# Sorted experts: block 0's results are gathered behind the scatters of the third part's rows

## The chip, the cores and the metric

The kernel runs on one core of a Trainium2 chip. The time is the device time of one execution in microseconds. The kernel before was run six times: 3030.4 to 3040.61 us, median 3032.41.

## The reference

Four layers act on 2048 tokens of 128 features. Each layer is a feed-forward part, an attention-like part, and the same feed-forward part again, all with residual sums. The change touches the boundary between layer 1 and layer 2: the second run of layer 1's feed-forward part, a mixture of 8 experts of which each token uses 2, and the feed-forward part of layer 2 that follows it.

```
def _L1_ffn_ref(x, rw1, rb1, rw2, rb2, we1, be1, we2, be2):
    ...
    logits = jax.nn.silu(xt @ rw1 + rb1) @ rw2 + rb2
    _, idx = jax.lax.top_k(logits, K)
    mask = jnp.zeros((n, E), bool).at[jnp.arange(n)[:, None], idx].set(True)
    w = jax.nn.softmax(jnp.where(mask, logits, -jnp.inf), axis=1)
    h = jax.nn.silu(jnp.einsum('nd,edh->enh', xt, we1) + be1[:, None, :])
    eo = jnp.einsum('enh,ehd->end', h, we2) + be2[:, None, :]
    y = xt + jnp.einsum('ne,end->nd', w, eo)
...
x = x + _L1_attn_ref(_layernorm(x, axis=-1), ...)
x = x + 0.5 * _L1_ffn_ref(_layernorm(x, axis=-1), ...)
x = x + 0.5 * _L2_ffn_ref(_layernorm(x, axis=-1), ...)
```

## The kernel before

The residual stream `x` stays in SBUF, features on partitions, as four blocks of 512 tokens. For the second run of layer 1's experts the class `Slots` sorts tokens by expert, so that each expert's tokens fill tiles of 128 rows and only the chosen experts are computed. The blocks form three parts: blocks 0 and 1 (23 tiles), block 2 (15 tiles), block 3 (15 tiles). "The third part" below is block 3; the code counts it as 2.

For each part the steps are these.

- `route` (from L1094 on) normalises a block, finds the two experts of each token and their shares, and turns the rows around (`s_xt`).
- `sort` works out a slot for each token and choice. Its first step adds the two choices (L1148); its second multiplies on TensorE (L1152, L1153); its third and fourth are small DVE operations (L1155 to L1175); its fifth writes the slots as integers (L1183) and issues eight scatters on GpSimd's queue (L1188), which write the rows of `s_xt` into `s_xd` in DRAM; its sixth finds each tile's expert (L1190 to L1194).
- `load` reads `s_xd` back, sorted, with four transfers on SyncE's queue (L1207).
- `body` and `part_of` run the tiles. Each tile has a first product (L1282, four matrix products into `s_h_ps`), a bias addition on DVE (L1287), a SiLU on ACT (L1288), and two tiles later a second product (L1298) into the sum bank `s_y`. There is one sum bank for four tiles; ACT copies it out (L1302) and SyncE stores it into `s_yd` in DRAM (L1303). Ahead of its use, DVE and ACT copy the expert's weights of each tile out of `we` (L1262). Every four tiles PE transposes the loaded rows (L1273) and ACT copies them (L1275).
- `combine(b)` brings the results of block b back to token order: eight gathers on GpSimd's queue (L1333) read `s_yd` into two tiles `s_g`; four transposes on PE (L1338) and a copy on ACT (L1340) turn the shares; 14 yields later DVE multiplies by the shares (L1345) and adds the two choices (L1346); 3 yields later PE multiplies the biases (L1349) and turns the sum (L1352); 2 yields later DVE adds it to `x` (L1355).

The order of all this is written by hand by `Weave`. The class runs a list of bodies (first the three parts of the sorted experts, then the gates and downs of layer 2's experts). After every `yield` of a body a clock advances by one, and `pump` first starts those waiting jobs whose conditions are met and then advances each active job whose time has come by one step. A job's yield of n puts its next step n clocks later, plus the job's slack: 2 by default, 0 where the job was given 0. At most two jobs with default slack run beside a body. The instructions of PE, DVE, ACT and GpSimd go into their queues in exactly the order in which this emits them; SyncE's order is found by the tile framework.

The jobs beside the sorted experts are set up in `in_slots`. `("sort", 0, 2)` is the third part's sort. Behind it come the load of `wg2`, the gate weights of layer 2 (2 MB, named `wg` in the profile, L1845), and `("loaded", 0, 2)`, the loads of the third part's rows. `("combined", 0, b)` is `combine(b)`; block 0's has slack 0. The condition of block 0's is that the body of the first part, `("slots", 0, 0)`, is through; each later block's combine waits also for the one before it. The first head of layer 2, `("head", 0, 0)` (normalisation L122 to L150, router L252 to L257, gate factors stored in DRAM as `rt_cd`), waits for `("combined", 0, 0)`; its factors are then spread by loads of 1 MB each into `f_xs` (L385), one while the sorted experts run and the next when their last buffers are free. DVE scales them (L1879) for the gate products (L1891).

Of the kernel before, what the change touches and what calls it, by code (L numbers as in the profile page):

```python
# [1713 lines left out]
class Behind:  # L1714
# [116 lines left out]
    def in_slots(self, weave):  # L1831

        fl, slots = self.fl, self.slots
        held = lambda name: fl.sp.tile([P, BLK], F32, tag="xn", name=name, bufs=3)
        weave.job(("loaded", 0, 0), [], lambda: slots.load(0, fl))
        weave.job("output", [("loaded", 0, 0)], lambda: self.fa.output(NB - 1, fl.sp, fl.bank, fl.work), 0)

        def load(*names):
            tiles = {name: self.late.tile(list(_SHAPES[name]), F32, tag=name, name=name) for name in names}
            for name, t in tiles.items():  # L1840

                flat = t.rearrange("p a b c -> p (a b c)") if len(t.shape) == 4 else t
                flat = t.rearrange("p a b -> p (a b)") if len(t.shape) == 3 else flat
                self.net.nc.vector.memset(flat[:, 0:1], 0.0)
                self.net.nc.sync.dma_start(t, self.net.ins[name])  # L1845
            self.w.update(tiles)
            return
            yield

        route = lambda: slots.route(3, fl.sp, fl.bank, fl.work, held)  # L1850
        weave.job(("route", 0, 3), ["output"], route, 0)
        weave.job(("loaded", 0, 1), ["output"], lambda: slots.load(1, fl), 0)
        sort = lambda: slots.sort(2, fl.bank, fl.work)
        weave.job(("sort", 0, 2), [("route", 0, 3)], sort, 0)
        weave.job("wg2", [("sort", 0, 2)], lambda: load("wg2"), 0)
        weave.job(("loaded", 0, 2), [("sort", 0, 2)], lambda: slots.load(2, fl), 0)
        weave.job("weights", [("slots", 0, 1)], lambda: load("wu2", "wd2", "rw3", "wg3", "wu3", "wd3", "wout3"), 0)
        weave.job("constants", [("combined", 0, 1)], self.constants)
        for b in range(NB):

            after = [("slots", 0, max(b - 1, 0))] + ([("combined", 0, b - 1)] if b else [])
            weave.job(("combined", 0, b), after, lambda b=b: slots.combine(b, fl), None if b else 0)


# [514 lines left out]
```

## Time and profile before

| | us |
|---|---|
| median of six runs | 3032.41 |
| the profiled execution | 3032.82 |
| its span | 3031.0 |
| PE busy | 2815.2 (93%) |
| DVE busy | 1937.0 (64%) |
| ACT busy | 1308.0 (43%) |
| POOL busy | 111.4 (4%) |
| first product of the second part's tiles (L1282) | starts at 1988.60 |
| slots of the third part written (L1183) | 1995.80, 0.19 long |
| load of `wg` issued (L1845) | 1997.81 |
| loads of the third part's rows issued (L1207) | 2025.79 |
| first product of the third part's tiles (L1282) | starts at 2039.40 |
| first gate product (L1891) | starts at 2081.12 |

Times within the execution count from the start of its span. PE is TensorE, DVE is VectorE, ACT is ScalarE, POOL is GpSimd and SP is SyncE. A row of a timeline gives start, duration, engine, source line, operation, the tile written and the tiles read, how many instructions were merged into it, and in brackets the engine's idle time before it with what ended that idle time. An fp32 matrix product shows as two matmul instructions, so eight stand for four products. A POOL row covers the work of building the transfer's descriptors, not the landing of its data.

### The profile page before, as it was taken

The numbers are of one execution on the slowest core, as the hardware profiler recorded it, in microseconds if no ns is written. First come the engines' busy times: TensorE is split into PE (matmuls) and PEld (weight loads), VectorE is DVE, ScalarE is ACT, GpSimd is POOL, SyncE is SP. The second block draws the span as 40 slices with busy tenths as digits, with TensorE's granted clock in tenths as the row PEclk, the third lists the DMA queues.
The fourth block names the chain that finished last, engine by engine and source line by source line (L and its number), as shares of the span: only waits on it lengthen the run. The fifth ranks groups of instructions, "written<-read, shape, count | busy, mean of one in ns | idle before, by whom it ended". The sixth has DMA issues, their size and how long they took to land.

```text
span 3031.0 us, 33081 instructions
## 1 busy us (share of the span) xinstructions
PE 2815.2 (93%) x12377; PEld 1239.9 (41%) x12404; DVE 1937.0 (64%) x3897; ACT 1308.0 (43%) x1717; POOL 111.4 (4%) x190
## 2 busy tenths in 40 slices
PE   6589999998899989999999999989999999999997
PEld 3234444443444432333333322576444444444443
DVE  4476686764545578999989886345355545553665
ACT  2365454532444425666666767754211122111242
POOL 0110000000000000000000001132000000000000
PEclk9789999998999988999999999989999999999998
DMA  1000100001001000000000001133221111110000
GB/s 51 4 1 1 47 1 1 1 1 58 15 1 42 22 22 15 6 21 17 7 27 6 14 5 39 38 100 138 85 75 65 70 56 70 56 75 37 28 1 15
DMA packets 53601, 101.03 MB, mean 33 GB/s; under 512 B 21572, under 2 KB 39752, under 8 KB 46784
## 3 DMA queue, kind: packets, MB, share of 16 engines
q1 hardware_dynamic: 51392, 94.71, 9.0%
q0 software_dynamic: 2048, 4.20, 0.5%
q8 instruction: 98, 1.61, 0.2%
q14 instruction: 63, 0.52, 0.1%
HBM read 83.35 MB, written 13.89 MB: 32 GB/s over the span
## 4 chain that ended last, share of the span: by engine, by line
PE 77%; DVE 14%; ACT 6%; issue 2%; DMA 1%; SPq 0%; another core or an unknown queue 0%; DVEq 0%; ACTq 0%; POOLq 0%
PE f_h L1891 15%; PE fa_av L1596 8%; PE fa_s L1530 8%; PE fa_s L1607 7%; PE f_y L1953 4%; PE f_y L969 4%; PE f_h_ps L960 3%; PE ga_u L832 3%; PE ga_u L842 3%; PE ga_s L816 3%; DVE fa_mx L1533 2%; PE f_y L521 2%; DVE f_ms L1936 2%; PE ln_c L122 2%; DVE ga_acc L658 1%
## 5 line engine op out<-in xcount | busy, mean ns | idle before, releaser
L1533 DVE TENSOR_REDUCE fa_mx<-fa_s 128x1 f32<-128x512 f32 x1024 | 652.1, 685 | 88.4 <-PE fa_s L1530 86.2
L1615 ACT ACTIVATE fa_ex<-fa_s 128x1024 f32<-128x1024 f32 x512 | 501.1, 1022 | 269.5 <-PE fa_s L1607 264.7
L1530 PE MATMUL fa_s<-fa_ks,fa_qs 75*128 75x512 bf16 x1024 | 366.1, 391 | 16.3 <-DVE fa_mx L1533 7.6
L1607 PE MATMUL fa_s<-fa_qs,fa_ks 75*128 75x512 bf16 x1024 | 308.5, 386 | 8.6 <-ACT fa_ex L1615 7.7
L1596 PE MATMUL fa_av<-fa_ex,fa_v 128*32 128x512 f32 x2048 | 277.4, 613 | 0.0
L1953 PE MATMUL f_y<-f_ms,wd 128*128 128x512 f32 x512 | 238.0, 602 | 12.0 <-DVE f_ms L1936 10.1
L1530 PEld LDWEIGHTS <-fa_qs 75*128 75x128 bf16 x1024 | 100.4, 98 | 316.3 <-issue 234.6
L1891 PE MATMUL f_h<-f_xs,wg 128*128 128x512 f32 x512 | 229.7, 595 | 0.0
L1891 PE MATMUL f_h<-f_xs,wu 128*128 128x512 f32 x512 | 226.2, 594 | 0.0
L1936 DVE TENSOR_TENSOR f_ms<-f_mid,f_xs 128x512 f32<-128x512 f32 x256 | 166.7, 687 | 15.0 <-PE f_y L1953 14.9
L1607 PEld LDWEIGHTS <-fa_ks 75*128 75x128 bf16 x1024 | 99.3, 99 | 133.0 <-issue 55.8
L1953 PEld LDWEIGHTS f_y<-f_ms,wd 128*128 128x128 f32 x512 | 91.6, 190 | 132.9 <-issue 80.0
L963 ACT ACTIVATE f_h<-f_h_ps,vec 128x512 f32<-128x512 f32 x128 | 87.2, 687 | 130.8 <-PE f_h_ps L960 128.0
L827 DVE TENSOR_TENSOR ga_a<-ga_s,ga_e 128x1024 f32<-128x1024 f32 x96 | 117.2, 1221 | 37.6 <-PE ga_s L816 22.1
L1891 PEld LDWEIGHTS f_h<-f_xs,wu 128*128 128x128 f32 x512 | 95.4, 190 | 111.9 <-issue 111.2
L966 DVE TENSOR_TENSOR f_h<-f_h,cb 128x512 f32<-128x512 f32 x128 | 86.0, 684 | 85.9 <-ACT f_h L963 74.5
L1891 PEld LDWEIGHTS f_h<-f_xs,wg 128*128 128x128 f32 x512 | 94.4, 190 | 107.2 <-issue 106.5
L960 PE MATMUL f_h_ps<-ln_xn,we 128*128 128x512 f32 x256 | 130.5, 595 | 1.1 <-DVE fa_f L1443 0.6
L1903 DVE TENSOR_TENSOR f_mid<-f_mid,f_h 128x512 f32<-128x512 f32 x32 | 22.0, 688 | 168.2 <-PE f_h L1891 168.2
L969 PE MATMUL f_y<-f_h,we 128*128 128x512 f32 x256 | 127.8, 593 | 0.0
L832 PE MATMUL ga_u<-ga_a,ga_kv 128*64 128x512 f32 x384 | 119.3, 634 | 3.0 <-DVE ga_state L801 2.0
L842 PEld LDWEIGHTS ga_u<-ga_xe,ga_diag 128*128 128x128 f32 x720 | 88.8, 194 | 75.8 <-issue 75.0
(466 smaller groups left out, 3754.5 us busy)
## 6 DMA issues: line engine op xcount, KB each, us to landing
f_xs<-rt_cd SPq DMA_DIRECT2D x48, 1024.0 KB
fa_ks<-fa_kd SPq DMA_DIRECT2D x48, 96.0 KB
fa_qs<-fa_qd SPq DMA_DIRECT2D x16, 288.0 KB
we<-in_we_dram SPq DMA_DIRECT2D x1, 4112.0 KB
s_x<-s_xd SPq DMA_DIRECT2D x11, 256.0 KB
s_yd<-s_ys SPq DMA_DIRECT2D x11, 256.0 KB
wg<-in_wg_dram SPq DMA_DIRECT2D x1, 2048.0 KB
wu<-in_wu_dram SPq DMA_DIRECT2D x1, 2048.0 KB
```

The costliest lines, as they stand in the source:

```text
L832: nc.tensor.matmul(u_ps[64 * h : 64 * h + 64, :], lhsT=kv[:, i, 2 * p + h, lo : lo + 64], rhs=a[:, h, :], start=True, stop=first, skip_gro ...
L842: nc.tensor.matmul(u_ps[:, r * P : (r + 1) * P], lhsT=now[:, r, int(step == 2), :], rhs=xe[:, r, :], start=False, stop=r == 3, skip_group_ ...
L960: nc.tensor.matmul(h_ps, lhsT=w["we"][:, e, 4 + c * P : 4 + (c + 1) * P], rhs=xn, start=True, stop=True)
L969: nc.tensor.matmul(y, lhsT=w["we"][:, e, 516 + c * P : 516 + (c + 1) * P], rhs=hs[e][:, c, :], start=False, stop=(e, c) == (7, 3),)
L1530: nc.tensor.matmul(s1, lhsT=qs[:, h, i * P : (i + 1) * P], rhs=ks[:, c, h, :], start=True, stop=True)
L1533: nc.vector.tensor_reduce(mx[:, h, i, c : c + 1], s1, AX.X, ALU.max)
L1596: nc.tensor.matmul(av[at], lhsT=v[:, n, at], rhs=exs[j // 2][:, j % 2, :], start=n == 0, stop=n == NT - 1)
L1607: nc.tensor.matmul(s2[:, j, :], lhsT=ks[:, n // 4, h, n % 4 * P : (n % 4 + 1) * P], rhs=qs[:, h, :], start=True, stop=True,)
L1615: nc.scalar.activation(ex, s2, AF.Exp)
L1891: nc.tensor.matmul(ps, lhsT=wt[:, e, c * P : (c + 1) * P], rhs=halves[e // 4][:, e % 4, :], start=e == 0, stop=e == 7,)
L1936: self.net.nc.vector.tensor_tensor(ms, mid[:, c, :], halves[e // 4][:, e % 4, :], ALU.mult)
L1953: nc.tensor.matmul(y, lhsT=self.w["wd2"][:, c, e, :], rhs=ms, start=e == 0 and c == 0, stop=e == 7 and c == 3,)
```

## The change

One condition of one job is added. Block 0's combine is to start only when the third part's sort is through, in addition to the first part's body. The instructions of both are the same; what changes is the order in which they, and those of the jobs that wait for block 0's combine, are put into the queues.

```diff
         for b in range(NB):
 
-            after = [("slots", 0, max(b - 1, 0))] + ([("combined", 0, b - 1)] if b else [])
+            after = [("slots", 0, max(b - 1, 0))] + ([("combined", 0, b - 1)] if b else [("sort", 0, 2)])
             weave.job(("combined", 0, b), after, lambda b=b: slots.combine(b, fl), None if b else 0)
```

## The prediction

> **What bounds the kernel now.** I read the page first (slices, the chain that ended last), then the timelines of POOL, PE, DVE, ACT and SP from 1975 to 2130 us, then that stretch in windows. The chain is the matrix engine's:
>
> ```profile
> span 3031.0 us, 33081 instructions
> ...
> PE 77%; DVE 14%; ACT 6%; issue 2%; DMA 1%; SPq 0%; another core or an unknown queue 0%; DVEq 0%; ACTq 0%; POOLq 0%
> ```
>
> So a change off PE counts only where PE waits. The sorted experts are such a place. What POOL does there (start, duration, line, idle before it):
>
> ```profile
> 1992.50 0.97 POOL L1333 DMA_INDIRECT s_g<-s_yd,s_slot  x1 [63.16 <-DVE s_w L1287]
> ...
> 2001.38 0.95 POOL L1333 DMA_INDIRECT s_g<-s_yd,s_slot  x1 [0.30 <-issue]
> 2002.63 1.00 POOL L1188 DMA_INDIRECT s_xd<-s_xt,s_slot  x1 [0.30 <-issue]
> 2007.00 0.98 POOL L1188 DMA_INDIRECT s_xd<-s_xt,s_slot  x1 [3.36 <-DMA s_xd<-s_xt,s_slot]
> ...
> 2023.51 0.96 POOL L1188 DMA_INDIRECT s_xd<-s_xt,s_slot  x1 [1.54 <-DMA s_xd<-s_xt,s_slot]
> 2024.77 0.98 POOL L1333 DMA_INDIRECT s_g<-s_yd,s_slot  x1 [0.30 <-issue]
> ...
> 2033.58 0.94 POOL L1333 DMA_INDIRECT s_g<-s_yd,s_slot  x1 [0.30 <-issue]
> ```
>
> Gathers run back to back, 1.25 us apart; each scatter waits for the one before to land, so about 2.5 us. The third part's scatters stand behind block 0's gathers although their slots were ready at 1995.99. SP's loads of the third part's rows (L1207) start at 2025.79, after the last scatter. Then PE halts. The chain of waits there:
>
> ```profile
> 2027.43 0.89 PE s_h_ps L1282 x8
> 2028.32 4.47 issue
> 2032.79 2.07 PE s_y L1298 x8
> 2034.86 1.55 PE s_x_ps L1273 x4
> 2036.41 0.04 DVEq L1287
> 2036.45 0.04 issue
> 2036.49 0.70 DVE s_w L1287
> 2037.21 0.64 ACT s_w L1288
> 2037.86 0.04 issue
> 2037.90 1.67 PE s_y L1298 x8
> 2039.56 0.91 PE s_h_ps L1282 x8
> ```
>
> From 2028.32 to 2039.56 PE does three products of 0.89 and four transposes of 0.44, 3.1 us at full clock, in 11.2: 8.1 us are lost, waits and half clock after them.
>
> **The change, step by step.** I count in ticks of the hand-written order, tick 0 being the yield after the first product of the second part. The sort of the third part steps at ticks 0, 1, 2 (scatters) and 3, and ends at 4. Before, block 0's combine starts at tick 0 with its gathers, multiplies at 14, has its matrix products at 17, adds to x at 19 and ends at 20; at 21 block 1's combine and the first head start. After, it waits for the sort: start 5, multiplies 19, products 22, add 24; block 1 and the head at 26. No instruction is added or removed. Moved are 8 gathers (POOL), 4 transposes and 6 products (PE), one copy (ACT) and 4 DVE operations, and everything queued on them.
>
> Scatters. A slot cast that ended at 1909.08 had its first scatter at 1909.84, 0.76 later. The cast here ends at 1995.99, less the 0.44 of the four transposes that leave PE's queue ahead of it: first scatter at 1996.3 instead of 2002.63. The eighth is seven steps of 2.505 later, 2013.8, if nothing disturbs. But SP sends the 2 MB of wg at 1997.81 in both kernels, and DMA is full until 2005.5. In the stretch 1999 to 2001 the queues moved
>
> ```profile
> q1 hardware_dynamic: 28, 0.46, 62.8%
> ```
>
> and nothing of POOL's q0, with gathers outstanding; q0 caught up in 2003 to 2007. So I let the second scatter (issued 1998.8) land only when wg is through: the third goes at 2005.5, not 2001.3, 4.2 us lost, and the eighth at 2018.0. Bounds: 0 lost, and 6.7 (4.2 and, for the next two, the 1.8 and 0.7 by which the first two waits of before exceeded 1.54). I take 4.2, since the q0 row is from this very place.
>
> The Trainium skill ("DMA: Bandwidth & Descriptors", Queues, rings and completion order) speaks against this delay: engines alternate between the queues packet by packet. By it a scatter would lose some 0.6 us (an estimate: one 16 KB packet at its 27 GiB/s), and the sum would be about 3.6 us smaller. The empty q0 row contradicts it, so the row is used.
>
> Gathers. Behind the eighth scatter the first follows after 1.26 and the eighth 8.81 later (2024.77 to 2033.58). The last landing: before, q0 emptied at about 2036, 2.4 after the issue. 2018.0 + 1.26 + 8.81 + 2.4 = 2030.5; bounds 2026.3 and 2033.0.
>
> Who waits. Before, DVE reached its multiplications (L1345) at 2014.33 without a wait: the gathers had landed by 2007. After, they stand behind the addition of tile 10 and one expert copy, which come some 2 us earlier than 2020.9, because PE's 2.1 us of combine products (L1349, L1352) no longer precede them: DVE is there at about 2018 and stops for 12 us. Behind it queue the bias additions of tiles 11 to 14 and the copies for tiles 13 and 14. PE gets through tile 12 and L1349 and stops at L1352 at about 2021.7. This new wait swallows the loss at 2028 (the rows' load now starts at 2018.0 + 2.28 = 2020.3 and is in before PE asks), but ends later than it.
>
> When PE goes on. Two multiplications 1.29, the sum 0.69, a handover of 0.1: 2032.6. To the third part's first product PE then has L1352 1.09, seven groups of 0.89 (products of tiles 13 and 14, second products of 10 to 14) 6.23, the next combine's transposes 0.44, ln_c 0.86, transposes of rows 0.44, ln_var 0.36: 9.42. After each halt here the granted clock is 0.5 for about 4 us (2032 to 2036 shows 0.52), which costs 2.05. 2044.1 against 2039.4 to 2039.56: +4.7, with the bounds of the landing +0.5 to +7.2.
>
> The third part. Block 1's multiplications and the head's router, 6.5 us of DVE, fall together before (2049.5 to 2057.7) and after (both five ticks on). Before, they stood in front of the copy that frees PE's sum bank (PE waited 3.82 at 2056.29); after, the bank is freed earlier, and tiles already expanded cover some: between -3.8 and 0, taken -1.5. The head is five ticks nearer to the end, so the first 1 MB of f_xs is issued at about 2077 and lands near 2082, when the second is on its way (before: 2066.04 and 2076.58). The second can then come 0 to 3 us late for the gate products, taken +1.5. Past that, blocks 1 to 3 shift by five ticks of 0.43 us each under products of 0.43; rows for the next gates were issued at 2123.3 for a use at 2145.9, 22 us ahead of a load of some 5 each. Nothing. SP: its stores of s_yd may stand behind the earlier loads; their only reader is block 2's gather, which waited until 2043. Nothing.
>
> Sum: +4.7 - 1.5 + 1.5 = +4.7. The profiled execution took 3032.82 us (3031.0 of it span), 0.4 above the median of 3032.41; on the median, 3037.1.
>
> **The rivals.** *The old loss returns behind the new wait* (slower). The halt of 2028 stopped DVE for 9.72 us at tile 14's addition, whose product had ended at 2028.3; the profile names no transfer it needed. If its cause is POOL's gathers beside a busy DMA, or the place in the instruction stream, it comes again after the restart, for block 1's gathers now follow block 0's at once. For: a similar DVE halt (4.84) stands at 1997.8 to 2002.6, also under gathers. Against: block 1's gathers would run with no large load beside them. Price 8.1: +12.8, 3045.2; it decides from 1.4 us of it on.
>
> *The wait is short and the third part smoother* (faster). Scatters lose nothing to wg (+0.5), PE comes back at full clock (-2.05), and the whole loss of 2052.47 to 2061.82 goes (9.35 for 3.9 of work: -5.45). -7.0, 3025.4. For: the rule above, and gathers of block 2 that now come later. Against: the q0 row, and the half clock after every halt.
>
> *It does nothing*: DVE gets to the multiplications so late that the gathers have landed. It would need a delay of 12 us before tile 10; the halts before it (1997.8, 2005.8) are there already. 3032.4.
>
> **How the numbers follow.** Chances: forecast 0.58, slower rival 0.26, faster rival 0.11, nothing 0.05. A change of 0.2% (6.1 us) is about what a measurement of this kernel tells from none. The forecast's own range is 3031 to 3041 (landing and third part together); about a quarter of it, 0.14, lies beyond +6.1. Slower 0.14 + 0.26 = 0.40; faster 0.10; same 0.50. For 8 in 10 the range reaches to the slower rival and halfway into the faster one: 3028.5 to 3045.5.
>
> **What would show it.** Scatters of L1188 starting near 1996, one step of about 6 us among them, the last near 2018; gathers of L1333 right behind, to about 2028; DVE idle some 12 us before L1345; PE idle some 11 us before L1352, half clock behind it; no 8 us loss before the third part's first product, and that product near 2044. Wrong if scatters step evenly through wg's load, if DVE has no wait at L1345, if a second halt follows, or if SP's loads don't move forward.

## The result, and the profile after

The changed kernel took 3045.68 us (median of 19 runs, 3035.49 to 3054.18) against 3035.09 for the kernel before (43 runs, 3022.16 to 3044.58): ratio 1.0036, 95% interval 1.0026 to 1.0046, which is 10.9 us slower (7.9 to 14.0). The profiled execution took 3042.17 us. Its page begins, and its chain that ended last reads:

```profile
span 3039.9 us, 33084 instructions
...
PE 26%; DVE 5%; ACT 0%; issue 0%; DVEq 0%
```

The span is 8.9 us longer. This chain can't be laid beside that of before: walked back, it breaks off at 2059.66, where the sorted experts' third part runs, so its shares add up to 31%. The timelines carry the reading instead. POOL's (start, duration, line, idle before it):

```profile
1998.91 0.96 POOL L1188 DMA_INDIRECT s_xd<-s_xt,s_slot  x1 [1.55 <-DMA s_xd<-s_xt,s_slot]
2005.77 1.11 POOL L1188 DMA_INDIRECT s_xd<-s_xt,s_slot  x1 [5.90 <-DMA s_xd<-s_xt,s_slot]
...
2018.41 0.96 POOL L1188 DMA_INDIRECT s_xd<-s_xt,s_slot  x1 [1.53 <-DMA s_xd<-s_xt,s_slot]
2019.68 0.98 POOL L1333 DMA_INDIRECT s_g<-s_yd,s_slot  x1 [0.30 <-issue]
...
2029.73 0.94 POOL L1333 DMA_INDIRECT s_g<-s_yd,s_slot  x1 [0.30 <-issue]
...
2038.72 0.95 POOL L1333 DMA_INDIRECT s_g<-s_yd,s_slot  x1 [0.30 <-issue]
```

The scatters start where the forecast put them: one step of 6.86 us (1998.91 to 2005.77) while the 2 MB of `wg` are under way, the eighth at 2018.41 (forecast 2018.0), block 0's gathers right behind, and block 1's gathers behind those at once, to 2039.67. PE in the same stretch:

```profile
2012.46 1.12 PE L1349 MATMUL s_y_ps<-s_ct,s_be2f 8*128 8x512 f32 x2
2032.60 2.07 PE L1352 MATMUL s_y_ps<-c,s_g 128*128 128x128 f32 x8 [19.02 <-DMA s_g<-s_yd,s_slot]
...
2043.59 1.13 PE L122 MATMUL ln_c<-x,center 128*128 128x512 f32 x2 [2.65 <-DVE x L1355]
...
2048.11 2.05 PE L1282 MATMUL s_h_ps<-s_xf,s_w 128*128 128x128 f32 x16
```

PE stops at L1352 for 19.02 us, not 11, because it gets there early, at 2013.6. It goes on at 2032.60, as forecast (2032.6). But the third part's first product comes at 2048.11, not 2044.1. DVE shows what lies between:

```profile
2029.82 0.69 DVE L1345 TENSOR_TENSOR s_g<-s_g,s_share 128x512 f32<-128x512 f32 x1 [19.64 <-DMA s_g<-s_yd,s_slot]
2031.13 0.69 DVE L1345 TENSOR_TENSOR s_g<-s_g,s_share 128x512 f32<-128x512 f32 x1 [0.62 <-DMA s_g<-s_yd,s_slot]
...
2033.54 0.67 DVE L1287 TENSOR_TENSOR s_w<-s_h_ps,s_w 128x512 f32<-128x512 f32 x1
...
2042.24 0.69 DVE L1287 TENSOR_TENSOR s_w<-s_h_ps,s_w 128x512 f32<-128x512 f32 x1 [7.70 <-issue]
```

The first two rows wait for the gathers, the second until about 2031.1. The last is the bias addition of tile 13. It stood idle for 7.70 us with nothing named as its releaser ("issue"), though the product it reads had started at 2036.17 and taken 1.91. It came 4.2 us late.

The trace also records when PE's semaphore rises. I measure from the start of the matmul that carries a signal to the next rise that the trace records; normally that is within 1.1 us. In this profile it was 4.5 us for the matmul at 2037.66, and 3.78 at 2074.12. I call that a late signal. The profile of before has them too, at 1994.7 to 2001.3 (up to 7.79 us), 2025.7 to 2028.1 (up to 3.54) and 2057.9 to 2059.6 (up to 3.81). In both kernels every one above 1.7 us stands within a burst of POOL's gathers or at most 0.1 us behind it.

The measure is rough. Between 1980 and 2100 us the seven profiles that have late signals in this stretch hold 855 to 1007 recorded semaphore updates, the other twelve 1298 to 1447. So rises may be missing from the record, and the next recorded rise need not be the one that belongs to the matmul. A delay is sure where the reader waits for it, as tile 13's addition does above. In the profile of before it is tile 14's addition, whose product carries its signal at 2028.05:

```profile
2036.49 0.69 DVE L1287 TENSOR_TENSOR s_w<-s_h_ps,s_w 128x512 f32<-128x512 f32 x1 [9.72 <-PE s_x_ps L1273]
```

It starts 8.4 us later, more than the 3.54 that the next recorded rise gives; the transposes that the row names (L1273) are not among what it reads.

### The profile page after: what moved, and what is told of

Same layout as the page of the kernel before. It is cut to its first block, busy times and chain, and to the rows that moved or that the text cites. A ratio compares the mean times of both kernels' runs of the same rounds, so it can differ in the third digit from the quotient of the medians.

```text
span 3039.9 us, 33084 instructions
## 1 busy us (share of the span) xinstructions
PE 2811.3 (92%) x12377; PEld 1235.8 (41%) x12404; DVE 1937.0 (64%) x3897; ACT 1308.8 (43%) x1718; POOL 111.6 (4%) x190
## 5 line engine op out<-in xcount | busy, mean ns | idle before, releaser
L1533 DVE TENSOR_REDUCE fa_mx<-fa_s 128x1 f32<-128x512 f32 x1024 | 652.1, 685 | 88.3 <-PE fa_s L1530 86.1
L1607 PEld LDWEIGHTS <-fa_ks 75*128 75x128 bf16 x1024 | 99.2, 99 | 132.1 <-issue 54.7
```

The source lines that it names most:

```text
L1533: nc.vector.tensor_reduce(mx[:, h, i, c : c + 1], s1, AX.X, ALU.max)
L1607: nc.tensor.matmul(s2[:, j, :], lhsT=ks[:, n // 4, h, n % 4 * P : (n % 4 + 1) * P], rhs=qs[:, h, :], start=True, stop=True,)
```

## The experiments

There were seventeen runs, in five groups; runs of a group share a chip. Three times are read from each profile: the second part's first product, the third part's first product and the first gate product (1988.60, 2039.40 and 2081.12 in the first profile of before). "Second" and "third" below are the two stretches between them; "to the gates" is their sum. Behind the gates before and after differ by no more than their repeats (before 946.7 to 952.9 us to the end, after 948.7 to 951.5).

| profile | late signals | second | third | to the gates |
|---|---|---|---|---|
| before, first | yes | 50.8 | 41.7 | 92.5 |
| after, first | yes | 59.6 | 43.1 | 102.7 |
| e1 after, block 1's combine later | no | 55.5 | 36.8 | 92.2 |
| e2 before, block 1's combine later | no | 45.1 | 37.1 | 82.2 |
| e3 after, wg later | no | 53.2 | 39.1 | 92.3 |
| e4 before, ticks moved alone | no | 46.6 | 38.9 | 85.5 |
| e5 before | no | 45.5 | 44.1 | 89.6 |
| e6 after | no | 54.7 | 39.0 | 93.8 |
| e7 before, wg later | no | 42.7 | 41.8 | 84.5 |
| e8 before, both later | no | 41.9 | 37.2 | 79.1 |
| e9 before | no | 46.8 | 41.5 | 88.3 |
| e10 after | no | 54.6 | 39.0 | 93.6 |
| e11 after, multiplications later | one, 1.45 us | 39.6 | 50.0 | 89.6 |
| e12 gathers between scatters | no | 39.9 | 38.1 | 78.0 |
| e13 before | yes | 50.5 | 41.6 | 92.1 |
| e14 after | yes | 61.2 | 41.5 | 102.7 |
| e15 before | yes | 50.3 | 41.6 | 91.9 |
| e16 after | yes | 59.6 | 43.2 | 102.8 |
| e17 after, block 1 by plain loads | in block 2's gathers | 56.5 | 40.0 | 96.5 |

**First group: is it block 1's gathers?** My first theory was that POOL's gathers make the halts, the rivals that the rows' load or the place in the instruction stream does.

e1 and e2 put one line behind the conditions of the change, in the kernel after and in the kernel before:

```diff
+            after += [("slots", 0, 1)] if b == 1 else []
```

> The kernel after, with block 1's combine held back until the second part's tiles are done, so that its eight gathers no longer run right behind block 0's. In the kernel after, PE goes on at L1352 at 2032.60 and the third part's first product starts at 2048.11. Theory 1 (block 1's gathers on POOL stop DVE at tile 13's bias addition until 2042.24, which costs PE about 4 us): the addition is through before 2039, and the third part's first product starts at 2044 or a little before (block 1's transposes, 0.44, are gone too). Theory 2 (the stop comes from the rows' load or the wake-up after the wait): the addition still ends near 2042, first product at about 2047.5. Theory 3 (it is tied to the place in the instruction stream): as theory 2. In all of them the third part gets block 1's combine and later heads on top, which may cost it 0 to 5 us, so that the whole time says less than the place: -4 to +1 us against the kernel after under theory 1, 0 to +5 under the others.

> The kernel before, with block 1's combine held back in the same way: no gathers between 2024.8 and 2034.5, where PE lost 8.1 us before the third part's first product at 2039.40. The load of the third part's rows (2025.79) stays where it was. Theory 1 (POOL's gathers stop DVE): DVE's addition of tile 14 ends before 2030 instead of 2037.2, and PE loses 0 to 2 us; first product of the third part near 2032. Theory 2 (the rows' load or its use of DMA): the stop stays, first product at 2038 to 2039.5. Theory 3 (place in the instruction stream): it stays too. The third part gets block 1's combine and later heads on top, 0 to 5 us, and it may meet the same stop there: the whole time is 0 to -7 us against before under theory 1, 0 to +5 under the others.

The premise failed in both. The line delays when block 1's gathers are put into POOL's queue order against other engines' work, but POOL has nothing else to do, so it ran them at once: in e2 the first starts at 2027.80, behind the last scatter at 2026.54. And yet neither profile has a late signal. So gathers alone don't make one, nor does the place in the stream: e2 is the kernel before up to tick 21, and the halt of 1997.8 is not there. e2 showed two other things. Without the halt PE waits 7.04 us at the turn of the third part's rows (L1273, for `s_x`), and the third part is shorter. Time: e2 0.9977 (0.9962 to 0.9991) of before, 7.0 us faster; e1 1.0029 (1.0013 to 1.0046), no gain on after: its shorter third part went with 955.5 us behind the gates instead of 951.

e3 holds `wg` back in the kernel after:

```diff
-        weave.job("wg2", [("sort", 0, 2)], lambda: load("wg2"), 0)
+        weave.job("wg2", [("slots", 0, 1)], lambda: load("wg2"), 0)
```

> The kernel after, with the 2 MB load of wg held back until the second part's tiles are done, so that the scatters of the third part's rows do not run beside it. The forecast's term (4.2 us lost to wg by one scatter): eight scatters step by 2.5 us, the last starts near 2013.9 instead of 2018.41, the gathers end near 2024, DVE multiplies at about 2025.5 and PE goes on at L1352 at 2028.2 instead of 2032.60; third part's first product 4.4 earlier, near 2043.7, if the stop at tile 13 comes as it did, and wg may then be late for the gates (start 2091.25). The other theory (the long step is POOL's own): the step of 6.9 us stays and so does all else. Whole time: -4 us against the kernel after, or 0; up to +5 if the gates wait for wg.

The 6.9 us step was gone, so it is `wg`'s; but the fifth scatter came 1.8 late (a step of 4.32) with none of SP's loads under way, and the stop at L1352 fell only from 18.6 to 16.28 us. Time 1.0012 (0.9999 to 1.0026), about 3.6 above before.

e4 leaves the gathers where they were in the kernel before, and moves only the ticks:

```diff
+        if b == 0:
+            yield 5
```

> The kernel before, with block 0's gathers left where they were (ahead of the scatters), and only the rest of its combine, and with it block 1's combine and the first head, five ticks later. This is the part of the change that shifts ticks without moving a gather. The forecast: costs nothing before the third part, and in the third part -1.5 + 1.5 = 0, so 0 within 2 us against before. Theory 1: block 1's gathers now start about 4 us later (when its combine does), so the stop of DVE moves with them, from 2026.8 to 2036.5 to about 2031 to 2040, and PE loses 6 to 10 us there; the third part costs +1.4 as in the kernel after (43.1 against 41.7). Theory 3 (place in the stream): the stop stays where it was.

The second stretch is that of before (46.6; e5 and e9 have 45.5 and 46.8), with a wait of 9.49 us at the turn of the rows. The third is 38.9, as after has it. So the shift of ticks by itself shortens the third part, and it is the move of the gathers that costs. Time 0.9993 (0.9978 to 1.0009), not told apart from before.

**Second and third group: the same kernels again.** e5, e6, e9 and e10 are before and after without an edit.

> The kernel before, unchanged, profiled once more. In its first profile the products' signals from PE reached DVE and ACT 3 to 8 us late at 1994 to 2002, 2025 to 2036 and 2058 to 2062; from the second part's first product (1988.60) to the third part's (2039.40) it took 50.8 us, and from there to the first gate product (2081.12) 41.7. The four kernels run since had no such late signal. Theory A (the late signals belong to the kernels before and after, where gathers run beside these products): they come back at the same places, 50.8 and 41.7 within 1 us. Theory B (they are chance, not of the kernel's order): they are not there, PE instead waits 9 to 10 us at the turn of the third part's first rows (L1273, for the load of s_x), and the two stretches take 46.6 and 39.0, as in the kernel with the ticks moved alone.

> The kernel after, unchanged, profiled once more. First profile: second part's first product 1988.52, third part's first product 2048.11, first gate product 2091.25: 59.6 and 43.1 us; DVE was 4.1 us late at tile 13's addition. Theory A (the late signal belongs to the kernel): again 59.6 and 43.1. Theory B (chance): 55.5 and 39 to 40, PE's wait at L1352 18 to 19 us as before, DVE at tile 13 in time. Under B the change costs 55.5 + 39.1 - 46.6 - 39.0 = 9 us against a kernel before that is free of late signals too, as under A; the ratio to before again 1.0036 within its interval.

> The kernel before, unchanged, a third profile. In the second there was no late signal of PE: the second part's first product to the third part's took 45.5 us with a wait of 6.55 at the turn of the third part's rows, the third part up to the gates 44.1 with a wait of 3.82 for s_ys. Late signals are chance: this profile is like the second, within 2 us at each stretch, unless it meets one, in which case it shows 3 us or more between a product's end and its reader at some other place than the first profile. Late signals are the kernel's: they stand where they stood in the first.

> The kernel after, unchanged, a third profile. Second profile: 54.7 us from the second part's first product to the third part's, with 18.64 of wait at L1352, then 39.0 to the gates. Chance: the same again within 2 us at each stretch; against the second and third profiles of before the second part costs +9, the third gives back 5, so about +4 in a clean pair, and the ratio by the clock lies between 1.0015 (the clean pair) and 1.0036 (the first measurement). The kernel's own: 59.6 and 43.1.

No late signal in any of the four. The clean kernel before has this chain of waits (e5):

```profile
2023.92 2.31 DMA s_xd<-s_xt,s_slot
...
2026.49 2.23 DMA s_xd<-s_xt,s_slot
2028.77 2.96 DMA s_x<-s_xd
2031.78 1.11 PE s_x_ps L1273 x4
```

The eighth scatter (2026.49) lands, the rows' load (2028.77) lands, PE turns the rows at 2031.78. Until then PE had waited 6.55 us. So the kernel before does lose time ahead of the third part without any halt: to the chain gathers, scatters, load. The halt of its first profile lay on top of that wait and was partly hidden in it. In the third part, before waits 3.82 us for the copy that frees the sum bank (e9, PE):

```profile
2057.02 2.08 PE L1298 MATMUL s_y<-s_w 128*128 128x128 f32 x8 [3.82 <-ACT s_ys L1302]
```

That wait stands in all five profiles of before and in none of after or of e4. Clean pairs: second stretch 54.65 against 46.15 (means), +8.5; third 39.0 against 42.8, -3.8; sum +4.7. Ratios 1.0022 (1.0010 to 1.0033) in the second group and 1.0031 (1.0014 to 1.0048) in the third: +6.7 and +8.4 us.

e7 is e3's edit on the kernel before, e8 has e2's and e7's edits together.

> The kernel before, with the 2 MB load of wg held back until the second part's tiles are done. Theory B (what sets the third part's start in the kernel before is gathers, then scatters, then the rows' load, and PE's wait for it): the second scatter steps 2.5 us behind the first instead of 5 to 6, the rows' load comes 3 to 4 us earlier, PE's wait at L1273 falls from 9.5 to about 6, the stretch from the second to the third part's first product is about 43 us, and the whole time 3 to 4 us below before. The rival (the long step is not wg's): no step is shorter, 46.6, 0 us.

> The kernel before, with both: wg held back and block 1's combine held back to the third part. Held back alone, block 1's combine gave -7.0 us (its products, 3 us of PE and its DVE work leave the second part's end, and the third part fills its own waits with them). If the two gains are of different kinds they add: about -10 us against before. If both only shorten the same wait of PE for the rows: block 1's later combine brings PE earlier to that wait, so that its gain must come from the third part alone and wg's from the wait; then -10 too. If the rows' load is no longer what PE waits for: -7 and PE's wait at L1273 near zero.

POOL in e7, first and second scatter:

```profile
2004.02 1.00 POOL L1188 DMA_INDIRECT s_xd<-s_xt,s_slot  x1 [0.30 <-issue]
2007.31 0.98 POOL L1188 DMA_INDIRECT s_xd<-s_xt,s_slot  x1 [2.29 <-DMA s_xd<-s_xt,s_slot]
```

The step is 3.3 us; in e5 it was 5.71. The rows' load is issued 35.2 us behind the second part's first product (e5: 38.2), PE's wait for the rows falls from 6.55 to 4.64, and the time to 0.9988 (0.9977 to 0.9999), -3.6 us as expected; as the fourth group will show, a time difference of that size alone proves little, so the shorter step and wait carry this reading. In e8 the gains add up only in part in the time: 0.9975 (0.9964 to 0.9986), -7.6 us, where -10 was expected and the profile's stretch is 9.9 shorter than the mean of e5 and e9.

e11 changes the kernel after:

```diff
-        yield 14
+        yield 14 if b else 28
```

> The kernel after, with block 0's multiplications, and all that follows them in its combine, 14 ticks later. If what costs is the place where DVE stands waiting for the gathers (bias additions of tiles 11 to 14 queue behind it, and PE stops 18.6 us at L1352), then here DVE and PE run through the second part without that wait: third part's first product about 38 us behind the second part's instead of 54.7, the rows being there, and DVE stops later, a few us, inside the third part; the first head comes 14 ticks later, which can cost the gates up to 8. Second part's first product to the first gate product 80 to 88 instead of 93.7, whole time 6 to 12 us below after. If the wait is set by something else (the rows' load, the scatters), PE stops as long at the turn of the third part's rows, and the time stays that of after.

The second stretch fell to 39.6: with the multiplications out of the way the 18.6 us stop is gone, so it is where DVE stands that made it. The rest of the expectation was wrong. PE, in e11:

```profile
2025.78 1.12 PE L1273 MATMUL s_x_ps<-c,s_x 128*128 128x128 f32 x4 [5.93 <-DMA s_x<-s_xd]
...
2080.49 3.78 PE L1891 MATMUL f_h<-f_xs,wg 128*128 128x512 f32 x4 [7.68 <-DVE f_xs L1879]
```

The rows were 5.93 us late for the turn, and the head, 14 ticks later, made the first gate products wait 7.68 us for `f_xs`. To the gates it is still 4 us shorter than after, but behind them it takes 958.6 us where after takes 948.7 to 951.5. Time 1.0054 (1.0033 to 1.0075), 16 us over before and the slowest of all: the later jobs cost more than the stop they avoid. What they cost behind the gates was not taken apart.

e12 starts from e8, takes block 0's gathers out of its combine, and issues them between the scatters:

```diff
+                if k == 2:
+                    one, *args = self.between.pop(0)
+                    one(*args)
...
+        if b == 0:
+            self.between = [(gather, i, j) for i in range(4) for j in range(2)]
...
-        yield 14
+        yield 14 if b else 22
```

> Neither order: block 0's gathers are issued one by one between the scatters of the third part's rows, in the 1.54 us that POOL waits for each scatter to land; with it wg held back, block 1's combine held back, and block 0's multiplications 8 ticks later than before. If a gather fits in that wait, scatters and gathers together take 20 to 28 us from the first scatter instead of 30, the rows' load is issued about 28 us behind the second part's first product (before: 38), PE's wait at the turn of the rows (4.2 in the kernel with both held back) goes, and the gates start 75 to 80 us behind the second part's first product (79.2 there): 0 to 4 us below that kernel, about -8 to -12 against before. If each gather holds the next scatter up (the landing comes later behind its packets), steps are 3.8 or more and nothing is gained: -7.

```profile
1999.12 0.98 POOL L1336 DMA_INDIRECT s_g<-s_yd,s_slot  x1 [0.30 <-issue]
2000.39 0.98 POOL L1188 DMA_INDIRECT s_xd<-s_xt,s_slot  x1 [0.30 <-DMA s_xd<-s_xt,s_slot]
2001.68 0.98 POOL L1336 DMA_INDIRECT s_g<-s_yd,s_slot  x1 [0.30 <-PE s_x_ps L1276]
```

Gather (L1336 there), scatter, gather: a gather fits into the wait of a scatter. From scatter to scatter it takes 2.54 to 2.64 us, once 3.62, against 2.5 without gathers; all sixteen are issued 21.3 us after the first starts (1997.85 to 2019.17). Time 0.9972 (0.9958 to 0.9986), 8.5 us faster than before, and not to be told from e8 or e2: block 0's products now wait 4.93 us at what is L1362 there. These three beat both kernels; their gains of 7.0 to 8.5 us are less than twice the 4.2 by which before differs from itself below, but to the gates their profiles are also 6 to 10 us shorter than the shortest of before.

**Fourth group: what is the rest?** In clean profiles the change costs +4.7, while the first measurement gave +10.9. What was open then: whether late signals make the rest, or the comparison is off.

> The kernel before, unchanged, timed against itself. If the comparison is sound, the ratio is 1 within its interval of about 0.0015 (5 us). If it lies beside 1 by 0.001 or more, the ratios of the other runs have an error of that size and the rest of 2 to 6 us needs no cause in the kernel. Profile: without late signals 88 to 90 us from the second part's first product to the first gate product, with them about 92.

> The kernel after, unchanged, a fourth profile on one more chip. If late signals make the rest: either this profile has them (99 to 103 us for the stretch) and the ratio is near 1.0036, or it has none (93 to 94) and the ratio is 1.0015 to 1.0022. If the ratio is near 1.0030 with no late signal here or in the next profile, the rest has another cause, which stays open.

> The kernel before, one more look at the same chip: the stretch 88 to 90 us without late signals, about 92 with them.

> The kernel after, one more look at the same chip: the stretch 93 to 94 us without late signals, 99 to 103 with them.

All four profiles have late signals, at the places of the first two. The two stretches together are 92.1 and 91.9 for before, 102.7 and 102.8 for after: +10.8. The bias addition of tile 13 in DVE's timeline, first in e6, which is clean:

```profile
2033.88 0.69 DVE L1287 TENSOR_TENSOR s_w<-s_h_ps,s_w 128x512 f32<-128x512 f32 x1 [2.69 <-issue]
```

and the same row of DVE's timeline in e14:

```profile
2042.70 0.69 DVE L1287 TENSOR_TENSOR s_w<-s_h_ps,s_w 128x512 f32<-128x512 f32 x1 [7.81 <-issue]
```

The idle time before it is 5.1 us longer.

So late signals come and go with the group of runs, not with the kernel. Where they are, the stretch to the gates is 9 us longer in after and 3 in before, whose wait of 6.6 us for the rows is gone in those profiles and so covers a part of them. The comparison is off too, by less: before against itself gave 0.9986 (0.9977 to 0.9995), -4.2 us where there is nothing to find. The ratio of after in this group was 1.0025 (1.0015 to 1.0034); against e13, the same kernel in the same group, its median is 10.9 higher (3043.58 and 3032.71). With late signals 1.0036 was expected, just outside that interval. By the clock the two kinds of group are not told apart: the ratios are 1.0036 and 1.0025 with late signals, 1.0022 and 1.0031 without. So that late signals make the rest of the first measurement is read from the profiles and not shown by the times.

**Last run: the gathers again.** In the kernel after, block 1's gathers are replaced by plain loads, which leaves out bringing block 1's rows back to token order:

```diff
+                if b == 1:
+                    row = (8 * j + first + i) * P
+                    nc.sync.dma_start(got[j][:, i * P : (i + 1) * P], self.yd[k][row : row + P])
+                    continue
```

> The kernel after, with block 1's eight gathers on POOL replaced by eight plain loads on SP of the same size (this leaves out bringing block 1's rows back to token order). On a chip with late signals: if POOL's gathers make them, the one at tile 13 (4.6 us, a few us behind L1352's start) is gone, the second part's stretch is 55 to 56 us instead of 59.6 to 61.2, and the later ones (in block 2's gathers) stay; if the restart makes it, it stays. On a chip without late signals: 54 to 55 us in either case, which tells nothing of their cause.

This run had late signals: up to 5.19 us at 2073.1 to 2076.9, in block 2's gathers, where after had them as well. The one at tile 13 was gone:

```profile
2043.30 0.69 DVE L1287 TENSOR_TENSOR s_w<-s_h_ps,s_w 128x512 f32<-128x512 f32 x1 [3.77 <-issue]
```

The idle time is 3.77 us instead of 7.7 to 7.8 (2.6 to 2.7 in the clean profiles), the third part's first product 12.3 us behind L1352's start, against 15.5 to 17.3 in the three profiles of after with late signals and 10.9 and 11.0 in the clean ones. It is one run, on a chip that by its number had shown none in the third group, so late signals don't seem to be a fixed property of a chip.

## Why the prediction was wrong, point by point

- **Scatters, wg, gathers, restart.** Right: 2018.41 for 2018.0, 6.86 for the step beside `wg`, L1352 at 2032.60. That the last fits to the hundredth is luck: the last gather landed at about 2031.1 instead of 2030.5, and one multiplication instead of two stood behind it. The empty queue row was the right thing to go by. The Trainium skill ("DMA: Bandwidth & Descriptors", Queues, rings and completion order) has engines alternate between queues packet by packet; the scatter step beside `wg` is 6.86 us in the first profile of after and 6.74 in e6, and 2.54 without it (e3), so here the measurement decides. Why none of the scatter's packets moved beside the load is not shown.
- **"DVE is there at about 2018 and stops for 12 us."** DVE was there at 2010 and stopped 19.64 us. The halts of before at 1997.8 and 2005.8, which the forecast kept, were late signals in a burst of gathers that the change moved away. It cost nothing, since the restart was set by POOL.
- **"This new wait swallows the loss at 2028."** This is the step that failed. The loss was not swallowed: in the first pair a second halt follows the restart, and the term of +4.7 up to the third part's first product measures +8.8 (59.6 less 50.8). The forecast took before with its late signals (50.8) and after without (2044.1 less 1988.5 is 55.6; clean profiles have 54.7 and 54.6). Either pair taken whole gives about twice the term: +8.5 clean, and +8.8 (first pair) or +10.0 (means of the fourth group's pairs, 60.4 and 50.4) with late signals on both sides.
- **The slower rival.** It was the right mechanism at half its price. The loss came back at tile 13 behind the restart: 2048.11 instead of 2044.1, 4.0 us of the 8.1. The argument against it, that no large load runs beside block 1's gathers, was wrong: the late signal stands there without such a load, and was gone in the one run without these gathers (e17).
- **The third part, -1.5 + 1.5.** In clean profiles it is -3.8 in the mean, with before's two profiles 2.6 apart (44.1 and 41.5): the wait of 3.82 goes entirely, near the lower end of the bounds given, and `f_xs` is not late. With late signals the third part gains nothing (+1.4 in the first pair), because after has another one, of 3.8 to 6.7 us, in block 2's gathers.
- **The sum.** +4.7 is also what the clean profiles show, but by two errors that cancel: +8.5 - 3.8. The times of the clean groups (+6.7, +8.4) hold it within their intervals; the first measurement, with late signals, does not (7.9 to 14.0), though the fourth group's ratio, with late signals too, does (+4.6 to +10.3). I had one profile of before and no way to see that a part of it comes and goes; the row with no releaser was the hint.

Not settled: what makes late signals come in one group of runs and not in another, how a gather delays PE's semaphore, and whether the lateness and the records that these profiles lack have one cause, the tracing among the candidates.

## What to carry to other kernels

A wait that the profile can't name may belong to the moment and not to the kernel: forecast both sides with it or both sides without it, and profile the kernel before a second time before it is subtracted. When a queue's two bursts change places, ask which of their readers comes first; here the gathers were wanted at tick 14 (19 in the changed kernel) and the rows only at the end of the part, and putting the gathers behind the scatters turned a 6.6 us wait for the rows into an 18.6 us wait for the gathers. Where one burst waits on itself, as the scatters do, the other fits in between (e12), and a 2 MB load can be sent later (e7, by its profile).

## What the runs showed of the hardware that was not expected

- A signal of PE reached its reader up to 8.4 us after the start of the matmul that carries it (tile 14 in before, 2028.05 to 2036.49). Seven profiles of nineteen have late signals, and these seven also record fewer semaphore updates; every signal of more than 1.7 us to the next recorded rise stood within a burst of POOL's indirect gathers or at most 0.7 us behind it. The readers then show "issue", or an engine long done, as the releaser.
- One indirect gather in the wait of an indirect scatter is nearly free: 2.54 to 2.64 us a pair, once 3.62, against 2.5 for the scatter alone.
- Before against before gave a ratio whose 95% interval leaves out 1 (0.9977 to 0.9995); differences of 0.15% of this kernel should not be read from one group.
